# A graph-attention and mixture-of-experts block: one weight fetch for two dense batches, and a different order of begun pairs at the end

## The chip, the cores and the metric

The kernel runs on one core of one Trainium2 chip. The time is the device time of one launch in microseconds (us). The core has engines with queues of their own that run in program order: PE (matrix products), DVE (vector work), ACT (activation functions), POOL (small vector work and the DMAs whose row numbers are data), and SP (plain DMAs). They wait for each other through semaphores. SBUF is the on-chip memory; PSUM holds what PE writes, in eight banks of 128 x 512 numbers here.

## The reference, cut to what matters

`x` is 64 batches of 256 rows of 256 numbers. Two layers are applied to every batch:

- layer 0: `x += elu(attention with 4 heads over adj)` and then `x += layernorm(x) @ W.T + b`
- layer 1: `x += relu(attention with 1 head over adj)` and then a mixture of eight experts with two chosen for each row:

```python
logits = tokens @ router_w.T                 # 8 numbers per row
rw, re = top_k(softmax(logits), 2)           # two experts and two weights, made to sum to 1
out = tokens
for e in range(8):
    h = gelu(tokens @ w1[e] + b1[e])
    out = out + combine[:, e:e+1] * (h @ w2[e] + b2[e])
```

All is float32. Tokens are normalized before every attention, feed-forward and expert stage; the result is 64 x 256 x 256 numbers.

## The kernel before, in words

**Routed batches and dense batches.** The first 62 batches are "routed". After a batch's layers, each of its rows is written twice to a buffer in device memory (`xs`), once in the region of each chosen expert (`send`, L877, an indirect DMA on POOL). Rows of one expert are then taken up in *pairs* of 128-row tiles, 256 rows each (`expert_pair`, L710): the pair is loaded by four DMAs (L726) and a small one for its weights (`xt`, L737), the expert's first weights and bias are fetched (`we`, 288 KB, L752), DVE turns the rows (`turned`, L116), PE and ACT form the hidden values (`hidden`, L783 and L789), PE multiplies by the second weights, which stay in SBUF (`result`, L798), DVE adds the bias and copies PSUM to a buffer `y` (L804), ACT multiplies each row by its weight (L776), and POOL adds the rows to the result in device memory (`scatter`, L815: two accumulating indirect DMAs of 128 rows each). The scatters of a pair wait for those of the pair before, since the same row can be in both. There are 131 pairs; below they are counted from 0 to 130. The last 14 (the flush) hold the incomplete remainders of each region, filled up by rows that point to the last batch.

The last two batches, 62 and 63, are "dense" (`dense_expert`, L831): all eight experts are applied to all their rows, with weights that are zero for experts not chosen; sums stay in SBUF (`base`) and are stored once. There each expert's weights are fetched once for each of the two batches. The result of the second matrix product goes to a `y` buffer with the bias added, and is then added to `base` by two DVE instructions (L843). The store of batch 63 comes after all scatters, because filling rows are added there.

**The order of the work** is written out by a small planner (L1042 to L1078). It counts steps, and three steps (TICKS) make up the time of one batch. Every piece of work is a generator; in each step every active one is advanced once, in the order of the ranks it yielded (low first), and a negative rank means once more in the same step. The order of these calls is the program order on all queues. The rules that matter here:

- A new batch is begun at steps 2, 5, 8 and so on, the last at step 191; its layers take 19 steps. `more` becomes false at step 194.
- In steps with step mod 3 = 1, waiting pairs are begun, against a credit: 2.0 more at each such step while there are new batches, 3.0 after that, 3.0 at most in store.
- A pair is loaded in the step it is begun (rank 90), fetches weights one step later, is turned another step later (rank 95), has its hidden product two steps after that (rank 30), its result one step later (rank 80), and is scaled in the next (rank 2). One pending pair is scattered in each step (rank 97).
- Two dense experts are begun in each step with step mod 3 = 2.
- `later` holds back parts of the routing of a chunk to certain steps of the three.

**Buffers**: seven for `we`, five for a pair's rows `xr`, seven for `y`, twelve for `xt`. A `y` buffer is free again when its scatter has landed, so the DVE instruction L804 can have to wait for a scatter.

Of the kernel before, what the change touches and what calls it, by code (L numbers as in the profile page):

```python
# [27 lines left out]
def kernel(  # L28
# [17 lines left out]
    nc = tc.nc  # L46
    B, N, D = x.shape
    E = router.shape[0]
# [3 lines left out]
    NT = N // P  # L52
# [194 lines left out]


    C_B1, WROW = KT * D, KT * D + 64
    WBUFS, XBUFS, YBUFS = 7, 5, 7  # L250
    wpack = tc.dram_tile([E, P, WROW], F32, name="wpack")
    w2s = const.tile([P, E, KT * D], F32, tag="w2s", name="w2s")
    b2s = const.tile([P, E, D], F32, tag="b2s", name="b2s")
# [158 lines left out]
    def projected1(xT, rstd, b):  # L412

        q = q1s[b % 2]
        pqs = []
        for t in range(NT):
            pq = bank("pq", [D + 3])
            for k in range(KT):
                nc.tensor.matmul(  # L419
                    pq, xT[:, k, t * P : (t + 1) * P], wx1[:, k, :],  # L420
                    start=(k == 0), stop=(k == KT - 1),
                )
            pqs.append(pq)
        ex = small.tile([P, NT, 3], F32, tag="ex1", name="ex1")
        for t, pq in enumerate(pqs):
            nc.scalar.activation(ex[:, t, :], pq[:, D:], AF.Exp, scale=rstd[:, t : t + 1])
            nc.scalar.activation(
                q[:, t, :D], pq[:, :D], AF.Copy, scale=rstd[:, t : t + 1]
            )
        me = work.tile([P, NT, N], F32, tag="me", name="me")  # L430
        for j in range(NT):
            nc.scalar.activation(me[:, j, :], masks[1][:, j, :], AF.Copy, scale=ex[:, j, 0:1])
        return q, ex, me
# [276 lines left out]
    def expert_pair(j, n, ids, ef, regs, needs):  # L710

        i = j % GROUP
        upto = min(j + GROUP, n)
        if i == 0:
            _, regs["e"] = nc.values_load_multi_w_load_instructions(
                ids[0:1, 0, j:upto], engines=[mybir.EngineType.SP], min_val=0, max_val=E - 1,
                skip_runtime_bounds_check_because=WHY,
            )
            _, regs["t"] = nc.values_load_multi_w_load_instructions(
                ids[0:1, 1, j:upto], engines=[mybir.EngineType.SP], min_val=0, max_val=E * CAP,  # L720
                skip_runtime_bounds_check_because=WHY,
            )
        e_sp, t_sp = regs["e"][i], regs["t"][i]
        xr = io.tile([P, PAIR // S, KT * S], F32, tag="xr", name="xr", bufs=XBUFS)
        loads = [
            nc.sync.dma_start(  # L726
                out=xr[g * S : (g + 1) * S],
                in_=xs_d.rearrange("(t c q) f -> t q c f", c=PAIR // S, q=S)[
                    bass.ds(t_sp, 1), :, :, g * KT * S : (g + 1) * KT * S
                ].rearrange("t q c f -> (t q) c f"),  # L730
            )
            for g in range(P // S)
        ]

        xt = small.tile([P, 2, ROW - D], F32, tag="xt", name="xt", bufs=12)
# [14 lines left out]
        yield 90  # L750
        we = io.tile([P, WROW], F32, tag="we", name="we", bufs=WBUFS)
        nc.sync.dma_start(  # L752
            out=we, in_=wpack[bass.ds(e_sp, 1), :, :].rearrange("e p c -> (e p) c")
        )
        yield 95
        xT = turned(work.tile([P, KT, PAIR], F32, tag="sT", name="sT", bufs=3), xr)
        w = small.tile([P, 2], F32, tag="w", name="w", bufs=8)
# [15 lines left out]
        y = result(hT, bass.ds(regs["x"][i], 1))  # L773
        yield 2
        for t in range(2):
            nc.scalar.activation(y[:, t, :], y[:, t, :], AF.Copy, scale=w[:, t : t + 1])  # L776
        scatters.append((y, xt))
# [13 lines left out]
            )  # L791
        return hT

    def result(hT, e):
        py = bank("py", [2, D])
        for t in range(2):
            for f in range(KT):
                nc.tensor.matmul(  # L798
                    py[:, t, :], hT[:, f, t * P : (t + 1) * P],
                    w2s[:, e, f * D : (f + 1) * D].rearrange("p e c -> p (e c)"),  # L800
                    start=(f == 0), stop=(f == KT - 1),
                )
        y = io.tile([P, 2, D], F32, tag="y", name="y", bufs=YBUFS)
        nc.vector.tensor_add(y, py, b2s[:, e, :].to_broadcast([P, 2, D]))  # L804
        return y
# [22 lines left out]
            tc.add_to_no_dep_group("out", d.ins)  # L828
            added.append(d.ins)

    def dense_expert(b, e):  # L831

        own = dense_batch[b]
        yield 90
        we = io.tile([P, WROW], F32, tag="we", name="we", bufs=WBUFS)
        nc.sync.dma_start(out=we, in_=wpack[e])
        yield 40
        yield 30
        hT = hidden(own["xT"], we)
        yield 80  # L840
        y = result(hT, slice(e, e + 1))
        for t in range(NT):
            nc.vector.scalar_tensor_tensor(  # L843
                own["base"][:, t, :], y[:, t, :], own["w"][:, t, e : e + 1],
                own["base"][:, t, :], op0=ALU.mult, op1=ALU.add,
            )
        if e == E - 1:
            while b == B - 1 and (scatters or len(added) < 2 * PAIRS):
                yield 99
            d = nc.sync.dma_start(  # L850
                out=out_rows[b * N : (b + 1) * N, :].rearrange("(t p) d -> p t d", p=P),
                in_=own["base"],
            )
            before = added[-2:] + based if b == B - 1 else []
            tc.declare_no_dep(
                d.ins, query=SYNC, group="out", keep=before,
                reason="no row is added to here, or every add is in their chain",
            )
            for ins in before:
                tc.add_manual_dep(d.ins, ins.name, AFTER, reason="filling rows were added here")  # L860
            tc.add_to_no_dep_group("out", d.ins)
            nc.sync.nop()


    active = []
# [3 lines left out]
    def begin(job, rank):  # L869
        active.append([rank, len(order), job])  # L870
        order.append(job)
# [16 lines left out]
    def later(rank, *phases):  # L888

        yield rank  # L890
        while order_steps[-1] % TICKS not in phases:
            yield rank

    def route(c, row0, nt, n, last, xng, lg):
# [101 lines left out]
    def route_dense(b, lg):  # L996
# [11 lines left out]
        )  # L1008
        nc.vector.tensor_tensor(w, ohs[:, 0], ohs[:, 1], ALU.add)
        dense_batch[b]["w"] = w  # L1010
        dense_jobs.extend(lambda e=e: dense_expert(b, e) for e in range(E))

    FLUSH = 2 * (E - 1)
    PAIRS = ROUTED * NT + E - 1
# [1 line left out]
    def jobs():  # L1016
        b = done = taken = 0
        for c, nb in enumerate(CHUNKS + (1,) * DENSE):
            nt = nb * NT
            lg = keep.tile([P, nt, E], F32, tag="lg", name=f"lg_{c}", bufs=10)  # L1020
            xng = []
            row0 = b * N
            done += nt
# [13 lines left out]

    batches = jobs()
    step, more, credit = 2, True, 0.0
    SETUP_AT = 3  # L1040
    with tc.manual_schedule():
        while more or active or waiting or dense_jobs or scatters:  # L1042
# [5 lines left out]
                    begin(nxt, 25)  # L1048
            if step >= SETUP_AT and setup:
                begin(setup.pop(0)(), 90)  # L1050
            if phase == 1:
                credit = min(credit + (2.0 if more else 3.0), 3.0)
                while waiting and credit >= 1.0:
                    credit -= 1.0
                    begin(waiting.pop(0)(), 90)
            if phase == 2:
                for _ in range(2):
                    if dense_jobs:
                        begin(dense_jobs.pop(0)(), 90)
            if scatters:  # L1060
                def one():
                    scatter()
# [51 lines left out]
```

## Time and profile before

| | us |
|---|---|
| three runs, median (lowest to highest) | 1665.73 (1664.08 to 1666.54) |
| the profiled execution itself | 1670.08 |
| its span in the profile | 1668.3 |
| busy: PE, DVE, ACT, POOL | 1495.5, 1317.4, 833.2, 889.4 |
| last product of the layers (L599) ends | 1419.2 |
| last product of a pair (L798) ends | 1635.8 |
| last scatter (L815) is issued | 1660.1 |

Times in the profile count from the start of its span. A group of instructions is named by engine, line, and what it writes and reads. In views of waits, the number is the time for which the first engine sat idle until the second one released it. The chain is the work followed back from the last instruction, at each step to what released it. A DMA that an engine issues through its queue lands later than its issue ends.

### The profile page before, as it was taken

What the parts mean: (1) busy time and instruction counts of PE and PEld (TensorE: products, weight loads), DVE (VectorE), ACT (ScalarE), POOL (GpSimd) and SP (SyncE); (2) the same over time, 40 slices, a digit from 0 to 9 for tenths busy, and PEclk for the clock granted to TensorE, in tenths of its full rate; (3) what the DMA queues carried; (4) which work ended last, traced back from release to release, by engine and by line L of the source; (5) the groups of instructions that cost most, each with busy time, mean ns of one, the idle gap of its engine ahead of it and who ended that gap; (6) DMA issues with size and microseconds to landing.
All of it is one profiled execution on the core that took longest, in us unless ns stands there. A gap on an engine that the chain in (4) does not pass through costs nothing.

```text
span 1668.3 us, 30242 instructions
## 1 busy us (share of the span) xinstructions
PE 1495.5 (90%) x8474; PEld 1311.2 (79%) x8474; DVE 1317.4 (79%) x4478; ACT 833.2 (50%) x1832; POOL 889.4 (53%) x853
## 2 busy tenths in 40 slices
PE   5898888899999999999999999999989987678782
PEld 4777777688888888888888888888878876567671
DVE  6888989999898988898989898998889876423330
ACT  0243444455656666666666665655555565323221
POOL 0121433545757575757575757574764666444344
PEclk8999999999999999999999999999999998879986
DMA  3812223255757575756575766665564676866753
GB/s 107 231 41 58 61 70 94 74 142 114 167 118 163 118 159 129 140 132 146 133 149 134 145 133 146 137 140 121 123 142 99 115 156 141 200 135 112 155 107 44
DMA packets 365285, 209.74 MB, mean 126 GB/s; under 512 B 264376, under 2 KB 335040, under 8 KB 365120
## 3 DMA queue, kind: packets, MB, share of 16 engines
q1 hardware_dynamic: 314496, 139.43, 34.0%
q0 software_dynamic: 49632, 67.39, 22.5%
q8 instruction: 70, 1.15, 0.3%
q10 hardware_dynamic: 992, 0.99, 0.2%
q14 instruction: 95, 0.78, 0.2%
HBM read 118.55 MB, written 89.15 MB: 124 GB/s over the span
## 4 chain that ended last, share of the span: by engine, by line
PE 55%; DVE 26%; DMA 6%; issue 5%; POOL 4%; ACT 2%; SPq 1%; DVEq 0%; POOLq 0%; ACTq 0%
PE ph L783 14%; PE pv L475 12%; PE py L798 9%; PE pq L384 5%; PE pq L419 4%; DVE z L461 4%; PE pf L529 4%; DVE stats L353 4%; DMA out_dram<-y,xt 3%; PE pt L368 3%; POOL out_dram L815 2%; DVE mv L354 2%; PE pl L599 2%; PE pd L454 1%; DVE x L535 1%
## 5 line engine op out<-in xcount | busy, mean ns | idle before, releaser
L815 POOL DMA_INDIRECT out_dram<-y,xt x262 | 416.7, 1591 | 255.4 <-DMA out_dram<-y,xt 73.0
L475 PE MATMUL pv<-q,z 128*128 128x65 f32 (+1 forms) x2560 | 369.8, 299 | 6.7 <-DVE z L461 5.3
L475 PEld LDWEIGHTS pv<-q,z 128*128 128x128 f32 x2560 | 331.9, 194 | 19.5 <-DVE z L461 5.8
L783 PE MATMUL ph<-sT,we 128*128 128x256 f32 x1048 | 259.1, 405 | 56.2 <-DVE sT L116 47.1
L361 POOL TENSOR_SCALAR rstd<-mv 128x4 f32<-128x4 f32 (+1 forms) x132 | 69.7, 528 | 436.1 <-DVE mv L354 352.9
L877 POOL DMA_INDIRECT xs<-xng,pos x248 | 251.1, 1012 | 69.2 <-issue 66.9
L783 PEld LDWEIGHTS ph<-sT,we 128*128 128x128 f32 x1048 | 209.8, 205 | 90.9 <-DVE sT L116 50.6
L798 PE MATMUL py<-w2s,hT 128*128 (+1 forms) x1176 | 263.9, 379 | 1.4 <-DVE z L461 0.7
L798 PEld LDWEIGHTS py<-w2s,hT 128*128 128x128 f32 x1176 | 219.7, 190 | 29.7 <-DVE z L461 1.0
L374 ACT COPY xT<-pt 128x512 f32<-128x512 f32 x192 | 113.3, 590 | 222.4 <-PE pt L368 184.7
L804 DVE TENSOR_TENSOR y<-py,b2s 128x512 f32<-128x512 f32 x147 | 97.5, 688 | 158.9 <-PE py L798 88.7
L789 ACT ACTIVATE hT<-ph,we 128x256 f32<-128x256 f32 x294 | 122.8, 471 | 183.3 <-PE ph L783 80.9
L461 DVE SCALAR_TENSOR_TENSOR z<-pd,q,mask 128x256 f32<-128x256 f32 x512 | 211.1, 473 | 0.3 <-PE pd L454 0.2
L362 POOL TENSOR_TENSOR rstd<-rstd,mhalf 128x4 f32<-128x4 f32 (+1 forms) x132 | 162.6, 1232 | 11.0
L776 ACT ACTIVATE y<-y,w 128x256 f32<-128x256 f32 x262 | 113.1, 501 | 104.4 <-DVE y L804 96.3
L353 DVE BATCH_NORM_STATS2 stats<-x 128x6 f32<-128x256 f32 x384 | 156.3, 407 | 2.2
L384 PE MATMUL pq<-wx,xT 128*128 128x268 f32 x512 | 137.9, 415 | 8.6 <-DVE wt L257 4.2
L419 PE MATMUL pq<-wx,xT 128*128 128x259 f32 x512 | 129.1, 394 | 15.5 <-ACT xT L374 11.2
L529 PE MATMUL pf<-wfT,xT 128*128 128x256 f32 x512 | 125.0, 388 | 0.0
L419 PEld LDWEIGHTS pq<-wx,xT 128*128 128x128 f32 x512 | 91.9, 189 | 41.9 <-ACT xT L374 22.4
L384 PEld LDWEIGHTS pq<-wx,xT 128*128 128x128 f32 x512 | 100.9, 202 | 30.1 <-issue 6.9
L551 ACT ACTIVATE rel<-pv,rinv 128x256 f32<-128x256 f32 x128 | 54.0, 474 | 108.2 <-DVE rinv L482 95.8
(151 smaller groups left out, 2233.8 us busy)
## 6 DMA issues: line engine op xcount, KB each, us to landing
we<-wpack SPq DMA_DIRECT2D x147, 288.0 KB
xr<-xs SPq DMA_DIRECT2D x524, 64.0 KB
xblk<-in_x_dram SPq DMA_DIRECT2D x256, 64.0 KB
xin<-in_x_dram SPq DMA_DIRECT2D x64, 256.0 KB
out_dram<-base SPq DMA_DIRECT2D x64, 256.0 KB
out_dram<-y,xt POOLq DMA_INDIRECT x262
xs<-xng,pos POOLq DMA_INDIRECT x248
xs<-fill SPq DMA_DIRECT2D x9, 260.0 KB
```

The source lines that it names most:

```text
L353: nc.vector.bn_stats(stats[:, t, :], src[:, t, :])
L362: nc.gpsimd.tensor_tensor(rstd[:, :n], rstd[:, :n], mhalf[:, :n], ALU.pow)
L384: nc.tensor.matmul(pq.rearrange("p h c -> p (h c)"), xT[:, k, t * P : (t + 1) * P], wx[:, k, :], start=(k == 0), stop=(k == KT - 1),)
L419: nc.tensor.matmul(pq, xT[:, k, t * P : (t + 1) * P], wx1[:, k, :], start=(k == 0), stop=(k == KT - 1),)
L461: nc.vector.scalar_tensor_tensor(z[:, j, :], pd[:, i, :], q[:, j, h, d + 2 : d + 3], mask[:, j, :], op0=ALU.max, op1=ALU.mult,)
L475: nc.tensor.matmul(pv[:, h, :], z[:, j, t * P : (t + 1) * P], q[:, j, h, : d + 1], start=(j == 0), stop=(j == NT - 1),)
L529: nc.tensor.matmul(pf[:, t, :], xT[:, k, t * P : (t + 1) * P], wfT[:, k, :], start=(k == 0), stop=(k == KT - 1),)
L783: nc.tensor.matmul(ph[:, f, :], we[:, k * D + f * P : k * D + (f + 1) * P], xT[:, k, :], start=(k == 0), stop=(k == KT - 1),)
L789: nc.scalar.activation(hT[:, f, :], ph[:, f, :], AF.Gelu, bias=we[:, C_B1 + f : C_B1 + f + 1])
L798: nc.tensor.matmul(py[:, t, :], hT[:, f, t * P : (t + 1) * P], w2s[:, e, f * D : (f + 1) * D].rearrange("p e c -> p (e c)"), start=(f == 0 ...
L815: d = nc.gpsimd.indirect_dma_start(out=out_rows, out_offset=bass.IndirectOffsetOnAxis(ap=xt[:, t, 0:1].bitcast(I32), axis=0), in_=y[:, t, ...
L877: d = nc.gpsimd.indirect_dma_start(out=xs_d[: E * CAP * PAIR, :], out_offset=bass.IndirectOffsetOnAxis(ap=at, axis=0), in_=xe, in_offset=None,
```

## The change

It has five parts. (1) A dense expert is one piece of work for both dense batches: one weight fetch, and then hidden product and result of batch 62 and, one step later, of batch 63. The jobs are begun once both batches are routed, one at every even step, instead of two at every third step. (2) Their results are not copied to `y`: DVE adds the PSUM product and the bias to `base` directly, in four instructions a batch and expert. The stores become jobs of their own. (3) From step 180 (DRAIN_AT) credit for pairs grows by 3.0, no longer from step 194. From step 209 (QUIET) one pair is begun in every step if fewer than three pairs wait for their scatter. (4) When there are no new batches, the turn of a pair has rank 75 rather than 95, and routing is no longer held back by `later`. (5) Buffers: `y` 7 to 9, `xt` 12 to 14, `w` 8 to 12, `me` 2 to 1, `lg` 10 to 7.

```diff
-    WBUFS, XBUFS, YBUFS = 7, 5, 7
+    WBUFS, XBUFS, YBUFS = 7, 5, 9
...
-        me = work.tile([P, NT, N], F32, tag="me", name="me")
+        me = work.tile([P, NT, N], F32, tag="me", name="me", bufs=1)
...
-        yield 95
+
+        yield 95 if more else 75
         xT = turned(work.tile([P, KT, PAIR], F32, tag="sT", name="sT", bufs=3), xr)
...
-    def result(hT, e):
+    def product(hT, e):
         py = bank("py", [2, D])
...
+        return py
+
+    def result(hT, e):
+        py = product(hT, e)
         y = io.tile([P, 2, D], F32, tag="y", name="y", bufs=YBUFS)
...
-    def dense_expert(b, e):
-
-        own = dense_batch[b]
+    def dense_expert(e):
+
         yield 90
         we = io.tile([P, WROW], F32, tag="we", name="we", bufs=WBUFS)
         nc.sync.dma_start(out=we, in_=wpack[e])
         yield 40
...
+        for b in range(ROUTED, B):
+            own = dense_batch[b]
+            yield 35
+            hT = hidden(own["xT"], we)
+            yield -85
+            py = product(hT, slice(e, e + 1))
+            for t in range(NT):
+                for add in (py[:, t, :], b2s[:, e, :]):
+                    nc.vector.scalar_tensor_tensor(
+                        own["base"][:, t, :], add, own["w"][:, t, e : e + 1],
+                        own["base"][:, t, :], op0=ALU.mult, op1=ALU.add,
+                    )
+            if e == E - 1:
+                begin(store_dense(b), 99)
...
-        while order_steps[-1] % TICKS not in phases:
+        while more and order_steps[-1] % TICKS not in phases:
...
-        dense_jobs.extend(lambda e=e: dense_expert(b, e) for e in range(E))
+        if b == B - 1:
+            dense_jobs.extend(lambda e=e: dense_expert(e) for e in range(E))
...
-            lg = keep.tile([P, nt, E], F32, tag="lg", name=f"lg_{c}", bufs=10)
+            lg = keep.tile([P, nt, E], F32, tag="lg", name=f"lg_{c}", bufs=7)
...
+    DRAIN_AT, QUIET = TICKS * (B - 4), TICKS * B + 17
...
-            if phase == 1:
-                credit = min(credit + (2.0 if more else 3.0), 3.0)
+            if step >= QUIET:
+                if waiting and len(scatters) < 3:
+                    begin(waiting.pop(0)(), 90)
+            elif phase == 1:
+                credit = min(credit + (2.0 if step < DRAIN_AT else 3.0), 3.0)
                 while waiting and credit >= 1.0:
                     credit -= 1.0
                     begin(waiting.pop(0)(), 90)
-            if phase == 2:
-                for _ in range(2):
-                    if dense_jobs:
-                        begin(dense_jobs.pop(0)(), 90)
+            if dense_jobs and step % DENSE == 0:
+                begin(dense_jobs.pop(0)(), 90)
```

More of the change, by code (lines that the diff above doesn't have):

```diff
@@ L733, in expert_pair @@
         ]
-        xt = small.tile([P, 2, ROW - D], F32, tag="xt", name="xt", bufs=12)
+        xt = small.tile([P, 2, ROW - D], F32, tag="xt", name="xt", bufs=14)
         loads.append(
@@ L754, in expert_pair @@
         )
-        yield 95
+        yield 95 if more else 75
         xT = turned(work.tile([P, KT, PAIR], F32, tag="sT", name="sT", bufs=3), xr)
-        w = small.tile([P, 2], F32, tag="w", name="w", bufs=8)
+        w = small.tile([P, 2], F32, tag="w", name="w", bufs=12)
         yield 30
@@ L837, in dense_expert @@
         yield 40
[L838 to L862, printed above, removed]
+        for b in range(ROUTED, B):
[12 more added lines that the diff above has]
+                begin(store_dense(b), 99)
@@ new lines, in store_dense @@
+    def store_dense(b):
+        own = dense_batch[b]
+        yield 99
+        while b == B - 1 and (scatters or len(added) < 2 * PAIRS):
+            yield 99
+        d = nc.sync.dma_start(
+            out=out_rows[b * N : (b + 1) * N, :].rearrange("(t p) d -> p t d", p=P),
+            in_=own["base"],
+        )
+        before = added[-2:] + based if b == B - 1 else []
+        tc.declare_no_dep(
+            d.ins, query=SYNC, group="out", keep=before,
+            reason="no row is added to here, or every add is in their chain",
+        )
+        for ins in before:
+            tc.add_manual_dep(d.ins, ins.name, AFTER, reason="filling rows were added here")
+        tc.add_to_no_dep_group("out", d.ins)
+        nc.sync.nop()
```

## The prediction

> **What bounds the kernel now.** I began with the busy shares over time (40 slices of 41.7 us, tenths):
>
> ```profile
> PE   5898888899999999999999999999989987678782
> ...
> DVE  6888989999898988898989898998889876423330
> ```
>
> Through slice 31 PE and DVE are full; in the last seven neither is, and in the last nothing is. The table by stage says when (columns: stretch, length, then busy time and instructions of PE, weight loads, DVE, ACT, POOL, granted clock, DMA share, GB/s):
>
> ```profile
> 1225.00:1320.00 95.00, 91.90 (x524) 81.41 (x523) 85.37 (x317) 54.25 (x117) 55.18 (x53) 0.96 0.52 109
> 1320.00:1430.00 110.00, 87.40 (x409) 75.24 (x408) 78.65 (x357) 59.01 (x124) 70.37 (x66) 0.89 0.74 160
> 1430.00:1636.00 206.00, 164.85 (x688) 139.75 (x688) 68.66 (x165) 64.43 (x146) 89.26 (x58) 0.89 0.67 128
> 1636.00:1668.30 32.30, 0.00 (x0) 0.00 (x0) 0.63 (x1) 0.91 (x2) 12.35 (x8) 0.58 0.35 45
> ```
>
> From 1430 on only pairs and dense experts are left, 238 us, and PE has 41 us of slack before its last product and then 32 us without work. So who sets the end? POOL's list in order of time, at its undisturbed end:
>
> ```profile
> 1651.90 1.54 POOL L815 DMA_INDIRECT out_dram<-y,xt  x1 [2.97 <-DMA out_dram<-y,xt]
> 1653.75 1.54 POOL L815 DMA_INDIRECT out_dram<-y,xt  x1 [0.30 <-issue]
> 1658.29 1.54 POOL L815 DMA_INDIRECT out_dram<-y,xt  x1 [2.99 <-DMA out_dram<-y,xt]
> ```
>
> A pair issues two scatters (1.85 apart), and the next pair starts 4.54 later, when they have landed: about 6.4 us a pair. From 1429.50 to 1658.29, in that list, 33 pairs start, 32 gaps, mean 7.15. Twenty-six gaps are 6.36 to 7.23 (mean 6.80; the 18 of them before 1600, with loads beside them, mean 6.92); six are 7.9 to 9.6. So the scatter chain sets the tail almost alone. The six long gaps show in the waits from 1430 to the end (total us, times, longest):
>
> ```profile
> POOL out_dram L815 <- DMA out_dram<-y,xt: 40.4, 12, 4.8
> PE ph L783 <- DVE sT L116: 39.6, 8, 9.8
> ...
> DVE y L804 <- DMA out_dram<-y,xt: 28.1, 8, 6.2
> ```
>
> and how they arise in the chain, in order of time (start, us, what):
>
> ```profile
> 1482.70 3.83 DMA out_dram<-y,xt
> ...
> 1486.65 0.70 DVE y L804
> ...
> 1489.69 0.72 DVE sT L116
> 1490.45 9.89 PE ph L783 x37
> ```
>
> A dense result wants a `y` buffer that a scatter still holds; the turns of the next three pairs stand behind it on DVE, PE starves and cools, the next pairs come late.
>
> [...] the trace has 2.97 after the issue has ended, and that is what I use. [...] 463 (L535) and 475 (L461) from PSUM, 482 (L843) from SBUF. [...] 24 hidden products take 5.45 us after 2.38 to 3.02 us idle, 8.28 after 9.83, but also 8.45 after 3.18.
>
> **The change, part by part.**
>
> *Pairs ahead.* I counted the planner's steps with the rules above. At step 178 two chunks become due, 12 pairs wait at step 179, and both kernels begin 3 at step 181. At steps 184, 187, 190 and 193 the old kernel begins 2 each, the new 3 each: 4 pairs more. At 196 to 208 both begin 3 every third step. So in step 209 the old kernel scatters pair 98 (its 1429.50), the new one pair 102. After it the old one has 32 pairs to scatter, one a step (last in step 241), the new one 28 (last in 238, with step 222 empty).
>
> *What the four pairs cost earlier.* Each is 8 + 8 products, 1.81 + 1.78 = 3.6 us of PE (5.45/3, 5.34/3), and 0.69 (L804) + 0.69 (L116) + 0.37 (L762, L766) = 1.75 us of DVE. They fall into 1225 to 1320, where PE has 3.1 us of slack in 95 and DVE 9.6. Between 4 x 1.75 = 7 us (PE's busy time there is stretched by waits: earlier batches take 21.4 us between base stores, these 24) and 4 x 3.6 = 14; I take 11. POOL gets 4 x 3.4 us of issue more; its own slack covers that in sum (55 of 95 busy), but it runs in order, and a norm can stand behind a waiting scatter, as here, where `rstd` is on the chain right behind one:
>
> ```profile
> 1350.36 1.55 POOL out_dram L815
> 1351.92 0.29 POOL rstd L361
> 1352.28 0.74 POOL rstd L362
> 1353.04 0.87 DVE x L535 x2
> ```
>
> Bounds: 0, and 4 x 6.45 = 26 if each extra scatter's cycle lengthens the layers; I take 3.
>
> *Routing not held, turns first.* From step 194 the routing steps move up by one or two (the fills from step 209 to 207). From 1320 to 1430 PE idles 22.6 us, largely because turns (rank 95) stand behind a chunk's small DVE instructions (1420.3 to 1427.6 is one such row, PE idle 6.84 before 1431.36). With rank 75 they stand ahead. Between 0 and 12 us back (nothing, or half the idle time; POOL's chain needs 6.45 of each of these steps of 8.4 us); I take 5. A turn ahead of L804 adds one wait: if rows are late, `y`, the scale and the scatter are late too. The load is two steps, 13 us, earlier and a load lands in 2 to 5 us, so 0; without that cover, the lateness goes straight into the chain.
>
> *The dense experts.* Eight fetches of 288 KB less, 2.36 MB, 18 us at 128 GB/s, in the shadow of other DMAs; eight SP issues fewer, with SP at some 3 us of each step (four row loads 1.9, `xt` 0.4, `we` 0.5, in SP's list). DVE per batch and expert: before 0.69 + 2 x 0.48 = 1.65, after 2 x 0.47 + 2 x 0.48 = 1.90; sixteen times, +4 us, hidden (DVE busy 69 of 206 us). They no longer take `y` buffers, and there are nine: PE may be nine pairs ahead of the scatters, where now it is seven buffers shared with the dense results. So the 28.1 us of DVE and with it the long gaps should go; the gap becomes that of an undisturbed pair with loads beside it, 6.92. Ends: 6.45 (undisturbed by loads) and 7.15 (as now).
>
> *One pair a step.* Does PE keep up? From step 209 it has 26 pairs and 16 dense units, 42 x 3.6 = 151 us at full clock, 170 at the 0.89 of now; 28 gaps of 6.92 are 194. In steps 215 to 230, with both, it needs 7.2 us for 6.92, so it gives back some 4 us of its lead of about 18 (two triples, 43 us of scatters in steps 209 to 214 for 22 us of PE). Covered.
>
> *Buffers.* `me` single: ACT writes (L432) at 1342.17 and next at 1360.54, DVE reads within a step of the first: 0; without that cover ACT, and the scales behind it, would wait part of a step. `lg`, `xt`, `w`: 0, their releases lie many steps back. A dense `we` lives 3 to 4 steps, so two of them and four of pairs take 6 of 7 buffers: no wait for SP, with the loads of the next pair queued behind it; a wait there would cost up to a step once.
>
> *Sum, against the profiled execution's span:* 1429.5 + 11 + 3 - 5 = 1438.5 for pair 102; + 28 x 6.92 = 193.8 gives 1632.3 for the start of pair 130; + 10.0 as now (1658.29 to 1668.3: second scatter, landing, store) = 1642.3. The median of the runs is 2.6 below this span, so 1639.7: **1640**, 1.5% faster. The likeliest case's own range is 1627 to 1651 (12 us either way: 7 to 14 for the pairs, 6.7 to 7.1 for the gap).
>
> **The rivals.**
>
> *The shift is worth more* (0.15): the layers cover the four pairs, turns give back 12, gaps of 6.6: 1429.5 + 0 + 185 + 10 - 2.6 = 1622. For it: PE and DVE idle from 1320. Against: before 1320 they don't.
>
> *The gap stays 7.15 and the layers pay all* (0.22): 1429.5 + 14 + 3 + 200 + 10 - 2.6 = 1654. For it: denser DMA traffic beside the scatters, 0.95 MB in each step of 7 us. Against: the six long gaps alone make up the 11 us by which the 32 exceed 6.80 each.
>
> *Slower* (0.10): POOL, in steps 184 to 208, with three scatters a batch. If in each of those eight batches a norm waits a whole scatter cycle, 6.45, the layers last 8 x 6.45 = 52 us longer: 1429.5 + 52 + 194 + 10 - 2.6 = 1683. It decides from about 35 us, 4.4 a batch. For it: the four lines above. Against: batches with three pairs today (the base stores at 1205.75 and 1230.20, 24.45 apart) last no longer than their neighbours (24.16, 24.19).
>
> *It doesn't matter* (0.03): the lead is lost again at PE, below a clock of 0.78, where 151 us become 194: 1663 to 1669. Now it is 0.89 with long idle times, which should shrink.
>
> **How the numbers follow.** The forecast has 0.50. Faster by over 0.2% (about what a measurement of this kernel can tell from no change) are the first three: 0.87; same 0.03; slower 0.10. For eight in ten I leave out the slower and unchanged cases and the lower half of the best: 1620 to 1660.
>
> **What would show it.** Right: pair 102 or so scattered when the last layer product ends; gaps near 6.9 with no run of 8 to 9; L804 hardly waiting for the scatter DMA; PE's waits for `sT` below 10 us in the tail; 139 fetches of `we`. Wrong: base stores over 27 us apart from 1250 on with POOL between them; gaps above 7.3; PE at a low clock. If SP turns out to wait for buffers in the tail, the loads bound the chain, and I have missed that.

## The result, and the profile after

| | before | after |
|---|---|---|
| median of four runs each, us (lowest to highest) | 1665.3 (1664.08 to 1666.54) | 1648.61 (1645.09 to 1651.53) |
| the profiled execution / its span | 1670.08 / 1668.3 | 1651.53 / 1649.6 |
| last `base` of batch 56 / of batch 63 (L574) | 1253.27 / 1400.89 | 1249.90 / 1416.02 |
| last product of the layers (L599) ends | 1419.2 | 1427.0 |
| first scatter of pair 102 / 119 / 130 | 1459.44 / 1583.74 / 1658.29 | 1443.07 / 1569.05 / 1639.68 |
| span's end after the last of these | 10.0 | 9.9 |

The ratio of the times is 0.9897, with a 95% interval of 0.9884 to 0.9911: 1.0% faster, where 1.5% was forecast. The two profiled executions lie further apart than the medians, since that of the kernel before took 4.8 us more than its median, that of the kernel after 2.9. Batches and pairs are counted from 0; `base` of a batch is what its layers hand to the routing, so its time marks the end of that batch's layers.

The busy shares over time of the kernel after (40 slices of 41.2 us, tenths of each slice; PEclk is the granted clock):

```profile
PE   5898888999999999999999999999989997599930
...
DVE  6888989999898989898989898999988877545510
...
PEclk8999999999999999999999999999999998799965
```

The dip of PE has moved to the slice at the end of the layers (5), and behind it PE is full until its work is finished. The table by stage (columns as before):

```profile
1225.00:1320.00 95.00, 93.19 (x525) 83.05 (x526) 85.79 (x306) 53.96 (x118) 52.53 (x50) 0.96 0.61 128
1320.00:1430.00 110.00, 88.44 (x441) 76.11 (x440) 78.63 (x361) 60.81 (x128) 77.32 (x70) 0.91 0.71 155
1430.00:1636.00 206.00, 140.16 (x636) 121.72 (x635) 71.74 (x169) 58.84 (x133) 90.78 (x59) 0.85 0.63 112
1636.00:1649.60 13.60, 0.00 (x0) 0.00 (x0) 0.00 (x0) 0.00 (x0) 3.69 (x3) 0.50 0.33 53
```

PE's clock of 0.85 from 1430 is a mean over work and idle time. The scatters of the tail split it better: the first row below runs from pair 102 to pair 119, the second from there to pair 130.

```profile
1443.07:1569.05 125.98, 124.80 (x569) 108.89 (x568) 62.48 (x149) 49.68 (x112) 52.80 (x35) 0.99 0.75 145
1569.05:1639.68 70.63, 11.85 (x55) 10.08 (x54) 4.90 (x12) 7.05 (x16) 33.95 (x23) 0.60 0.36 41
```

In the first row PE is busy 99% of the time at a granted clock of 0.99, and yet it isn't what most of the scatters wait for. L799 issues 280 products in it and 32 after it, eight to a result: 16 dense results and 19 of pairs in the first row, 4 of pairs after it. So 23 of pairs are left to multiply when 28 pairs are left to scatter, and 4 when 11 are left. PE draws away from POOL while it is full.

The waits of the kernel after from 1430 to the end (total us, times, longest):

```profile
POOL out_dram L820 <- DMA out_dram<-y,xt: 64.8, 19, 5.4
...
DVE y L809 <- DMA out_dram<-y,xt: 10.0, 2, 5.7
...
PE ph L784 <- DVE y L809: 9.6, 1, 9.6
```

The first line can't be set against the 40.4 of before. The view puts many of the waits of a scatter down to whatever else ended at that moment, even to loads of weights (`we`, 8.4 in the kernel after) that a scatter doesn't use, and a second profile of the same kernel has 48.5 in this line. Under all names together POOL's waits before L820 are 118.8 us here and 134.9 before; the gaps between scatters, below, are the better measure. DVE's wait for a `y` buffer has fallen from 28.1 to 10.0, and PE's for the turn `sT` (39.6 before) is no longer among the large ones: 2.2 us, once, before 1442.

POOL in order of time, in the loaded part and at the end:

```profile
1503.35 1.54 POOL L820 DMA_INDIRECT out_dram<-y,xt  x1 [3.32 <-DMA out_dram<-y,xt]
1505.19 1.54 POOL L820 DMA_INDIRECT out_dram<-y,xt  x1 [0.31 <-issue]
1511.12 1.54 POOL L820 DMA_INDIRECT out_dram<-y,xt  x1 [4.38 <-ACT hT L790]
...
1633.21 1.54 POOL L820 DMA_INDIRECT out_dram<-y,xt  x1 [2.93 <-DMA out_dram<-y,xt]
1635.06 1.54 POOL L820 DMA_INDIRECT out_dram<-y,xt  x1 [0.30 <-issue]
1639.68 1.54 POOL L820 DMA_INDIRECT out_dram<-y,xt  x1 [3.07 <-DMA out_dram<-y,xt]
```

The pair at 1503.35 needs 7.77 us, the one at 1633.21 needs 6.47. The gaps from 102 to 119 have a mean of 7.41 (125.98/17), those from 119 to 130 of 6.42 (70.63/11). In the kernel before the same pairs have 7.31 and 6.78 (124.30/17 and 74.55/11). So only the last eleven gaps have become shorter, those that now run when PE's work is done.

**Where the 18.7 us between the spans come from.** Batch 56 is 3.4 earlier (1253.27 to 1249.90; the second profile of the kernel after, below, has 1246.18, so this term is uncertain by that much). From there to the last `base` the layers take 166.1 instead of 147.6: 18.5 lost. From the last `base` to pair 102 there are 27.05 instead of 58.55: 31.5 gained. The chain from 102 to 130 takes 196.6 instead of 198.85: 2.2 gained. The end is 0.1 shorter. Sum 3.4 - 18.5 + 31.5 + 2.2 + 0.1 = 18.7. So the lead in pairs pays, and more than half of it is paid for in the layers. What makes them 15 us later?

### The profile page after: what moved, and what is told of

Read it like the earlier page. It is cut to its first block, busy times and chain, and to the rows that moved or that the text cites. A ratio compares the mean times of both kernels' runs of the same rounds, so it can differ in the third digit from the quotient of the medians.

```text
span 1649.6 us, 30216 instructions
## 1 busy us (share of the span) xinstructions
PE 1476.3 (89%) x8474; PEld 1299.8 (79%) x8474; DVE 1323.8 (80%) x4494; ACT 831.0 (50%) x1832; POOL 889.4 (54%) x853
## 3 DMA queue, kind: packets, MB, share of 16 engines
q0 software_dynamic: 49632, 67.39, 22.8%
## 4 chain that ended last, share of the span: by engine, by line
PE 62%; DVE 21%; DMA 5%; POOL 4%; issue 3%; ACT 3%; SPq 1%; DVEq 0%; POOLq 0%; ACTq 0%
PE pv L475 14%; PE ph L784 13%; PE py L799 12%; PE pq L384 5%; PE pq L419 5%; PE pf L529 4%; DVE z L461 3%; PE pt L368 3%; DVE stats L353 3%; DMA out_dram<-y,xt 3%; POOL out_dram L820 2%; PE pl L599 2%; DVE mv L354 2%; ACT xT L374 1%; PE pd L454 1%
## 5 line engine op out<-in xcount | busy, mean ns | idle before, releaser
L820 POOL DMA_INDIRECT out_dram<-y,xt x262 | 415.4, 1585 | 241.1 <-DMA out_dram<-y,xt 87.6
L361 POOL TENSOR_SCALAR rstd<-mv 128x4 f32<-128x4 f32 (+1 forms) x132 | 71.0, 538 | 432.2 <-DVE mv L354 337.1
L799 PE MATMUL py<-w2s,hT 128*128 (+1 forms) x1176 | 266.1, 379 | 1.3 <-ACT hT L790 1.2
L784 PE MATMUL ph<-sT,we 128*128 128x256 f32 x1048 | 242.8, 385 | 11.8 <-DVE y L809 9.6
L799 PEld LDWEIGHTS py<-w2s,hT 128*128 128x128 f32 x1176 | 219.5, 190 | 30.0 <-ACT hT L790 2.2
L784 PEld LDWEIGHTS ph<-sT,we 128*128 128x128 f32 x1048 | 198.9, 194 | 38.5 <-issue 9.9
L461 DVE SCALAR_TENSOR_TENSOR z<-pd,q,mask 128x256 f32<-128x256 f32 x512 | 211.1, 473 | 0.3 <-PE pd L454 0.2
L362 POOL TENSOR_TENSOR rstd<-rstd,mhalf 128x4 f32<-128x4 f32 (+1 forms) x132 | 163.0, 1235 | 11.0
L809 DVE TENSOR_TENSOR y<-py,b2s 128x512 f32<-128x512 f32 x131 | 85.8, 686 | 68.6 <-PE py L799 48.8
L529 PE MATMUL pf<-wfT,xT 128*128 128x256 f32 x512 | 124.1, 386 | 0.0
```

Of the source, the lines that this page charges most:

```text
L362: nc.gpsimd.tensor_tensor(rstd[:, :n], rstd[:, :n], mhalf[:, :n], ALU.pow)
L461: nc.vector.scalar_tensor_tensor(z[:, j, :], pd[:, i, :], q[:, j, h, d + 2 : d + 3], mask[:, j, :], op0=ALU.max, op1=ALU.mult,)
L529: nc.tensor.matmul(pf[:, t, :], xT[:, k, t * P : (t + 1) * P], wfT[:, k, :], start=(k == 0), stop=(k == KT - 1),)
L784: nc.tensor.matmul(ph[:, f, :], we[:, k * D + f * P : k * D + (f + 1) * P], xT[:, k, :], start=(k == 0), stop=(k == KT - 1),)
L799: nc.tensor.matmul(py[:, t, :], hT[:, f, t * P : (t + 1) * P], w2s[:, e, f * D : (f + 1) * D].rearrange("p e c -> p (e c)"), start=(f == 0 ...
L820: d = nc.gpsimd.indirect_dma_start(out=out_rows, out_offset=bass.IndirectOffsetOnAxis(ap=xt[:, t, 0:1].bitcast(I32), axis=0), in_=y[:, t, ...
```

## The experiments

The theory after this reading: the four pairs cost the layers time because POOL runs in order, and the small norm instructions (`rstd`, L361 and L362) stand behind their waiting scatters. Its rival: the pairs' products and turns take the time of PE and DVE, as the forecast had it. A second dispute: what shortens the tail, the lead or the single edits to its order, buffers and fetches. A ratio is that to the kernel before on the same chip, with its 95% interval; all edits are to the changed kernel.

### One repeat, and the early drain undone

**The changed kernel again**, unedited:

> The changed kernel itself, as the measure for the other runs of this series: ratio to the kernel before 0.988 to 0.991, last base (ACT, L574) 14 to 16 us later than in the kernel before. Both theories expect the same.

Measured: 1649.9 us, ratio 0.990 (0.9873 to 0.9926). In its profile the marks are 1.0 to 3.7 us earlier: batch 56 1246.18, last `base` 1412.93, pair 102 1441.55, pair 130 1638.66. Differences of that size between two profiles are not read as effects below. It is the yardstick for the profiles below.

**No early drain**, all else as changed:

```diff
-    DRAIN_AT, QUIET = TICKS * (B - 4), TICKS * B + 17
+    DRAIN_AT, QUIET = TICKS * B + 2, TICKS * B + 17
```

> The changed kernel, but three pairs a batch only from step 194 on, as before; step 209 then scatters pair 98 rather than 102. Theory (the lead of four pairs is what pays): the tail has 32 gaps instead of 28, 28 us more, and the layers lose 11 to 18 us less: 10 to 17 us slower than the changed kernel, 1658 to 1666. Rival (the layers pay the lead back, and the gain comes from the dense experts having left the y buffers): within 3 us of the changed kernel's 1648.6.

Measured: 1656.3, ratio 0.9929 (0.9906 to 0.9951), span 1656.9. The last `base` is at 1395.01, and pair 102 at 1452.86. So the early drain moves pair 102 by 9.8 (1452.86 to 1443.07): from the last `base` to pair 102 it saves 30.8 (57.85 to 27.05), and the layers give back 21.0 (1395.01 to 1416.02). The chain from 102 to 130 takes 194.2 here against 196.6, which leaves 7.3 between the spans and about 5 between the medians' ratios, whose intervals just overlap; by time alone its worth is barely shown. The drain isn't the whole of the gain: without it the kernel is 11.4 us of span below the one before, of which 4.0 lie before batch 56, 1.8 in the layers after it, 0.6 from the last `base` to pair 98, 4.8 in the chain from pair 98 to 130 (228.8 to 224.0), and 0.2 at the end.

### What the four pairs cost: scatters or products

**The same four pairs (86, 89, 92, 95), not scattered.** They are loaded, turned and multiplied; their rows are not added to the result.

```diff
+        begun.append(j)
+        mine = len(begun) - 1
...
-        scatters.append((y, xt))
+        if mine not in SKIP:
+            scatters.append((y, xt))
...
+    begun, SKIP = [], (86, 89, 92, 95)
```

> The changed kernel, with the scatters of pairs 86, 89, 92 and 95 left out (the third pair of four batches; their rows are missing in the result), all their other work kept. Theory (in the last batches the layers wait for POOL, whose queue is held by one scatter cycle in every step, and with it for sends and norms): the last base comes 12 to 20 us earlier than in the changed kernel, and the time falls by as much. Rival (the extra products and vector work are the price): 0 to 5 us earlier.

**The same four pairs, scattered but without products.** Their `y` is zeroed by DVE instead.

```diff
-        hT = hidden(xT, we)
+        hT = hidden(xT, we) if mine not in SKIP else None
...
-        y = result(hT, bass.ds(regs["x"][i], 1))
+        if mine in SKIP:
+            y = io.tile([P, 2, D], F32, tag="y", name="y", bufs=YBUFS)
+            nc.vector.memset(y, 0.0)
+        else:
+            y = result(hT, bass.ds(regs["x"][i], 1))
```

> The changed kernel, with the products and activations of the hidden layer and the result of pairs 86, 89, 92 and 95 left out; a DVE memset of y stands in for L809, loads, scales and scatters stay. Theory (POOL is the price): the last base moves by less than 5 us. Rival (PE is the price, 4 x 3.6 us): 9 to 15 us earlier, and the time falls by as much.

Measured: without scatters 1633.59, ratio 0.9798 (0.9777 to 0.9819); without products 1652.68, ratio 0.9918 (0.9901 to 0.9936), no faster than the repeat beside them. The last `base` in ACT's list in order of time, in the repeat:

```profile
1412.93 1.08 ACT L574 ACTIVATE base<-x,by 128x256 f32<-128x256 f32 x2
```

without scatters:

```profile
1397.15 1.08 ACT L574 ACTIVATE base<-x,by 128x256 f32<-128x256 f32 x2
```

and without products:

```profile
1413.83 1.08 ACT L574 ACTIVATE base<-x,by 128x256 f32<-128x256 f32 x2
```

So leaving out the products ends the layers no earlier, and leaving out the scatters ends them 15.8 us earlier, 4 a pair. Pair 102 comes 15.8 earlier too (1425.79), and the time is 16.3 lower: the whole of it reaches the end. The chain of the kernel after shows how (start, us, what):

```profile
1355.69 1.61 POOL out_dram L820
1357.30 0.30 issue
1357.60 1.58 POOL out_dram L820
1359.19 0.29 POOL rstd L361
...
1359.55 0.74 POOL rstd L362
...
1360.31 0.88 DVE x L535 x2
```

and the waits near the end of the layers (1330 to 1420) count it. The kernel before:

```profile
DVE by L560 <- POOL rstd L362: 6.7, 3, 4.4
...
DVE x L535 <- POOL rstd L362: 2.5, 1, 2.5
```

The repeat:

```profile
DVE by L560 <- POOL rstd L362: 16.3, 3, 8.3
...
DVE x L535 <- POOL rstd L362: 7.3, 2, 5.9
```

Without the products:

```profile
DVE by L560 <- POOL rstd L362: 16.7, 3, 8.8
...
DVE x L535 <- POOL rstd L362: 10.6, 2, 8.2
```

Without the scatters:

```profile
DVE by L560 <- POOL rstd L362: 7.0, 2, 6.9
```

DVE's wait for `rstd` falls from 23.6 to 7.0 us when the scatters go, and stays (27.3) when the products go: 16.6 us, near the 15.8 by which the layers end earlier.

That is not the whole of the price, though. Cut at the `base` of batch 60, the layers after batch 56 show two stretches (columns as before). The kernel before:

```profile
1253.27:1344.42 91.15, 87.08 (x506) 77.33 (x505) 78.93 (x296) 53.28 (x115) 53.79 (x52) 0.98 0.54 113
1344.42:1400.89 56.47, 47.47 (x219) 40.93 (x218) 40.25 (x190) 32.83 (x70) 37.79 (x37) 0.88 0.77 160
```

The kernel after:

```profile
1249.90:1347.58 97.68, 96.29 (x562) 86.20 (x561) 86.24 (x315) 58.88 (x130) 59.62 (x56) 1.00 0.61 129
1347.58:1416.02 68.44, 49.88 (x243) 42.53 (x241) 42.58 (x213) 32.83 (x72) 48.45 (x44) 0.90 0.68 137
```

Without the four scatters:

```profile
1245.76:1343.44 97.68, 96.29 (x562) 86.23 (x561) 86.92 (x318) 58.94 (x130) 57.89 (x57) 1.00 0.61 128
1343.44:1397.15 53.71, 46.68 (x243) 41.21 (x241) 41.48 (x213) 33.02 (x71) 38.24 (x37) 0.96 0.75 157
```

Without the products:

```profile
1246.68:1341.83 95.15, 88.56 (x513) 78.01 (x511) 85.09 (x316) 55.77 (x121) 58.49 (x55) 0.98 0.62 127
1341.83:1413.83 72.00, 49.73 (x228) 42.33 (x227) 43.40 (x215) 32.94 (x71) 50.89 (x47) 0.87 0.71 138
```

Of the 18.5 us that the layers lose, 6.5 are lost before batch 60 and 12.0 after it. Before batch 60 PE is busy for 96.29 of 97.68 us at a granted clock of 1.00, with 9.2 us more of work than in the kernel before; leaving out the scatters changes nothing there, and leaving out the products shortens the stretch by 2.5; what the other 4.0 are is not shown. After batch 60 the scatters decide: DVE waits 21.9 us for `rstd` (15.9 and 6.0) instead of 9.2, 12.7 more, near the 12.0. The time won without products before batch 60 is lost again behind the scatters (72.00), so it doesn't show at the end of the layers. The two prices don't add up: with the scatters gone, the layers after batch 56 still take 151.4 us, against 147.6 in the kernel before and 145.8 without the early drain.

**The norms taken off POOL**, the cause in another way: all scatters stay, but from step 194 on `rstd` is formed by ACT as exp(-0.5 ln(variance + eps)), with `eps_c` a constant tile.

```diff
+        if order_steps and order_steps[-1] >= TICKS * B + 2:
+            nc.scalar.activation(rstd[:, :n], mv[:, :n, 1], AF.Ln, bias=eps_c)
+            nc.scalar.activation(rstd[:, :n], rstd[:, :n], AF.Exp, scale=-0.5)
+            return
```

> The changed kernel, with the two POOL instructions of a norm (L361, L362) replaced from step 194 on by two on ACT, exp(-0.5 ln(var + eps)); each brings up to two table loads of 1.28 us, and ACT was busy 47 of 80 us between 1320 and 1400. Theory (of POOL's price, most comes from norms that stand behind a scatter waiting for its turn): DVE no longer waits for rstd for 16 + 7 us between 1330 and 1420, the last base comes 5 to 14 us earlier, and the time falls by 3 to 12 us. Rival (sends that stand behind scatters are the price, and pair loads wait for them): the last base within 4 us of the changed kernel's, or later by ACT's loads.

Measured: 1641.17, ratio 0.9848 (0.9828 to 0.9869), which lies below the changed kernel's interval (0.9884 to 0.9911): the fastest here that leaves nothing out. The last `base` of this kernel:

```profile
1395.95 1.10 ACT L580 ACTIVATE base<-x,by 128x256 f32<-128x256 f32 x2
```

It is 17 us earlier than in the repeat, with all four pairs scattered, and DVE waits for no `rstd` from 1330 to 1442. This run takes all late norms from behind all scatters, not only those of the four pairs, and the norms' own time off POOL; the kernel before with its norms off POOL was not run. That the four pairs' scatters are the cause rests on the run without them; this one adds that it is the order on POOL rather than the scatters' traffic, which is all still there. Only half comes out at the end: pair 102 at 1434.94 is 6.6 earlier. POOL still has the same sends and scatters in its order, and PE now waits for weights (19.0 us for `we` from 1330 to 1442); which of the two holds the rest back was not tested. The rest is 2.8 us in the chain (102 to 130 takes 194.35). The table by stage of this kernel shows what fills the time:

```profile
1320.00:1400.00 80.00, 74.36 (x387) 65.26 (x386) 66.11 (x306) 69.60 (x136) 57.34 (x48) 0.98 0.74 151
```

The changed kernel's row of the same stretch:

```profile
1320.00:1400.00 80.00, 67.35 (x347) 58.46 (x346) 58.72 (x260) 46.77 (x101) 59.01 (x54) 0.94 0.67 140
```

PE gets 7 us more work done in these 80, and ACT, with room before, takes up 22.8 us more: more work in the stretch, the norms, and a table load of 1.28 us each for the logarithm and the exponential.

### Is the tail the scatter chain's?

**One scatter a pair from pair 102 on**, so the second 128 rows of each of these pairs are not added.

```diff
-        for t in range(2):
+        scattered.append(y)
+        for t in range(2 if len(scattered) <= 102 else 1):
```

> The changed kernel, with only the first of the two scatters of each pair from pair 102 on (half of their rows are missing in the result). Theory (the scatter chain sets the whole tail): the undisturbed gap falls from 6.43 by the 1.85 between the two issues to about 4.6, and the time by 40 to 52 us, until PE's last product (1581) plus some 12 us is reached. Rival (PE or the loads set the part of the tail with dense experts, where the chain of the profile runs through PE from 1442 to 1574): 15 to 25 us less, from the last eleven gaps alone.

Measured: 1598.5, ratio 0.959 (0.9555 to 0.9625), 51 us below the repeat. POOL in order of time:

```profile
1537.91 1.54 POOL L821 DMA_INDIRECT out_dram<-y,xt  x1 [5.37 <-ACT y L777]
1544.82 1.54 POOL L821 DMA_INDIRECT out_dram<-y,xt  x1 [5.36 <-ACT y L777]
...
1563.81 1.54 POOL L821 DMA_INDIRECT out_dram<-y,xt  x1 [3.64 <-ACT y L777]
1568.26 1.54 POOL L821 DMA_INDIRECT out_dram<-y,xt  x1 [2.91 <-ACT hT L790]
1572.75 1.54 POOL L821 DMA_INDIRECT out_dram<-y,xt  x1 [2.95 <-ACT hT L790]
```

With one scatter an undisturbed gap is 4.45 to 4.49. (This kernel was timed twice only, 1594.99 and 1602.01.) The gaps around 1540 are 6.91, and end with the scaling of `y`, which has to wait for products: there PE has become the bound, with a pair and a dense unit in each gap (busy 28.00 of the 28.00 us from 1531 to 1559). So the chain bounds the tail of the changed kernel, but PE stands only 0.5 us a gap behind it (6.91 against 7.41).

### The single parts, undone one at a time

**Two fetches again** (one for each dense batch, the second a step later):

```diff
-        for b in range(ROUTED, B):
+        we2 = io.tile([P, WROW], F32, tag="we", name="we", bufs=WBUFS)
+        nc.sync.dma_start(out=we2, in_=wpack[e])
+        for b, we in zip(range(ROUTED, B), (we, we2)):
```

> The changed kernel, with the dense weights fetched twice again, 8 x 288 KB more while scatters run. Theory (scatters land later when loads run beside them, 7.2 to 7.4 a gap against 6.43; what the single fetch saves is in that): 2.36 MB more beside 17 loaded gaps, about a seventh more load traffic, so a seventh of their 16 us of excess: 1 to 4 us slower. Rival (the fetches are hidden): within 1 us. Third possibility (SP waits for a free weight buffer and pair loads come late behind it): 5 us or more slower.

Measured: 1647.18, ratio 0.9891 (0.9868 to 0.9915). The table of this kernel for the stretch with dense work:

```profile
1430.00:1570.00 140.00, 129.53 (x587) 112.98 (x588) 68.11 (x159) 53.57 (x121) 58.65 (x38) 0.96 0.82 163
```

and of the changed one:

```profile
1430.00:1570.00 140.00, 129.26 (x587) 112.46 (x587) 67.74 (x161) 52.15 (x118) 58.39 (x38) 0.96 0.75 146
```

The DMA share is 0.82 instead of 0.75, at 163 GB/s instead of 146, and from 102 to 119 it takes 124.1 against 126.0. The fetch saved is worth nothing that these runs can tell, and its bytes don't set the gap.

**Dense results through `y` again**, and, in another kernel, **seven `y` buffers**:

```diff
-            py = product(hT, slice(e, e + 1))
+            y = result(hT, slice(e, e + 1))
...
-                for add in (py[:, t, :], b2s[:, e, :]):
-                    nc.vector.scalar_tensor_tensor(
-                        own["base"][:, t, :], add, own["w"][:, t, e : e + 1],
-                        own["base"][:, t, :], op0=ALU.mult, op1=ALU.add,
-                    )
+                nc.vector.scalar_tensor_tensor(
+                    own["base"][:, t, :], y[:, t, :], own["w"][:, t, e : e + 1],
+                    own["base"][:, t, :], op0=ALU.mult, op1=ALU.add,
+                )
```

> The changed kernel, but dense results go through a y buffer (one bias addition, two additions to base) as before; nine buffers, one weight fetch for both batches. Theory of the prediction (dense results in the y buffers made the long gaps): 4 to 10 us slower, DVE waiting for the scatter DMA over 25 us in the tail. Rival (with the pairs one a step and nine buffers it does not matter, DVE stalls are hidden by PE's lead): within 2 us.

```diff
-    WBUFS, XBUFS, YBUFS = 7, 5, 9
+    WBUFS, XBUFS, YBUFS = 7, 5, 7
```

> The changed kernel with seven result buffers instead of nine. Theory (the scatter chain bounds, PE is far ahead, and dense results no longer take buffers): within 2 us of 1648.6. Rival (the two buffers are needed to keep the chain fed): 4 us or more slower, with DVE waiting for scatters for over 25 us in the tail.

Measured: 1648.68, ratio 0.989 (0.986 to 0.992), and 1651.6, ratio 0.9902 (0.9877 to 0.9926). The waits from 1430 on in the kernel with dense results through `y`:

```profile
DVE y L809 <- DMA out_dram<-y,xt: 48.8, 11, 7.9
```

and in the kernel with seven buffers:

```profile
DVE y L809 <- DMA out_dram<-y,xt: 40.6, 9, 6.4
```

These waits are longer than the 28.1 of the kernel before and the 15.7 of the repeat. Pair 130 starts at 1638.58 and 1639.02 all the same (1638.66 in the repeat). With a lead, DVE's wait for a buffer was here the scatter chain pushing back, not what made it slow.

**Turns last again**, **routing held again**, and **groups of three to the end**:

```diff
-        yield 95 if more else 75
+        yield 95
```

> The changed kernel, but the turn of a pair keeps rank 95. Theory of the prediction (turns first give back 5 us): 3 to 8 us slower than 1648.6. Rival (a turn that waits for late rows holds up the bias addition behind it, and the layers): 2 to 6 us faster.

```diff
-        while more and order_steps[-1] % TICKS not in phases:
+        while order_steps[-1] % TICKS not in phases:
```

> The changed kernel, but routing is held to its steps to the end, as before. Theory (the layers end 15 us later because sends and routing crowd together on POOL and DVE in the last batches, and pair loads then wait for fresh sends): base (ACT, L574) of the last batch 4 us or more earlier than 1416, and 3 to 8 us faster than 1648.6. Rival (three scatters a batch are the cause): the last base stays within 3 us of 1416, and the time stays within 3 us or grows by one step, 7 us.

```diff
-    DRAIN_AT, QUIET = TICKS * (B - 4), TICKS * B + 17
+    DRAIN_AT, QUIET = TICKS * (B - 4), TICKS * B + 999
```

> The changed kernel, but pairs are begun three at a time at every third step to the end, as before. Step count: the last pair is scattered in step 237 rather than 238. Theory (the scatter chain sets the tail as long as it is fed, whatever the order of begun pairs): within 3 us of the changed kernel. Rival (beginning one a step is what removes the long gaps): 5 us or more slower, with several gaps over 8 us between 1480 and 1600 as in the kernel before.

Measured: 1654.19, ratio 0.9902 (0.987 to 0.9934); 1652.49, ratio 0.9906 (0.9881 to 0.9931); 1650.81, ratio 0.9914 (0.9884 to 0.9945). The last `base` stands at 1415.95, 1414.66 and 1414.52 (the kernel after 1416.02), pair 130 at 1645.51, 1638.98 and 1636.22. None of the three is told from the changed kernel by its time. In the profile of the first the tail is 6 us longer, which its ratio doesn't bear out.

## Why the prediction was right, and where it was not

The direction and the order of the gain were right: 1648.61 is within 1620 to 1660 and within the likeliest case's own 1627 to 1651, 8.6 above 1640. Against the sum's own terms: pair 102 at 1443.1 for 1438.5 (+4.6), 28 gaps of 7.02 for 6.92 (+2.8), the end 9.9 for 10.0, and the median 1.0 below the profiled span instead of 2.6 (+1.6). The sum of these is 8.9.

Part of this closeness is luck. The 9 us that the sum allowed for the layers (11 + 3 - 5) were 18.5 from batch 56 on, 9.5 more. They became +4.6 because batch 56 came 3.4 earlier, which was not forecast, and because the way from the last `base` to the pair at this place was 1.6 shorter (28.61 to 27.05).

- **Pairs ahead: held.** After the layers' last product the new kernel goes on to scatter pair 100, the old one pair 97: three ahead by the clock, four by the count of steps, in which 102 stands where 98 had.
- **"What the four pairs cost earlier": the terms were the wrong way round.** 3 for POOL was 15.8, by the run without scatters. The 11 for PE and DVE has an answer only in part: up to batch 60, where PE is full, 6.5 us are lost and the scatters have no share in them, but without the products the layers end no earlier, because the scatters' delay covers that. The likeliest case had named the mechanism, a norm behind a waiting scatter, and its bound of 0 to 26 held the value, but "its own slack covers that in sum" failed: POOL was idle for 32.7 of the 110 us from 1320 to 1430 in the kernel after, and still the four pairs' scatters delayed norms: DVE waited 23.6 us for `rstd` in the repeat and 7.0 without them. The rival "slower" priced the same mechanism at 6.45 in each of eight batches; measured, the layers lose 18.5 in all, 2.3 for each of its eight batches, below the 4.4 where it would have decided. The mark given for it, base stores more than 27 apart, isn't there either: 25.2 at most. The delay is uneven: 1.2 to 2.5 us a batch up to batch 60, 6.4 in the next one.
- **"I take 5" for turns first and routing not held: not found.** Undoing either leaves the last `base` within 1.4 us. The idle time of PE from 1320 to 1430 is 21.6 against 22.6. More of it hangs on POOL and the norms than on the rank of the turns: from 1320 to 1400 PE idles 12.7 us in the changed kernel and 5.6 with the norms off POOL.
- **The gap of 6.92: the rule failed, the size nearly held.** The mark "gaps above 7.3" came in the loaded part (7.41), 6.42 came in the unloaded part, and the mean of 7.02 lay between the ends of 6.45 and 7.15. That the mean of two kinds of gap comes near the 6.92 for all is luck. The long gaps did not go with DVE's waits: from pair 98 on there are seven of 7.9 or more, six before. Their explanation by `y` buffers falls with the two kernels above, which have more of those waits and no longer tail.
- **The dense experts and one pair a step at nothing: held.** There are 139 fetches of `we`, and neither the second fetch nor groups of three change the time. DVE's additions to `base` took 481 ns each with the product from PSUM and 485 with the bias from SBUF; in the kernel before the means are 464 and 473 for L535 and L461 with a source in PSUM, and 482 for L843 from SBUF.
- **PE keeps up: held, for a smaller lead.** It was to lose 4 us of an 18 us lead to gaps of 6.92; since the gaps were 7.41 it gained. At 6.92 it would have been level with the 6.91 that the kernel with one scatter shows for it.
- **SP waiting for buffers: not found as such**, but the loads of pairs wait for fresh rows: 31.0 us in 1330 to 1442 for the sends (`xs`), 10.6 before in a longer stretch (1180 to 1435). Fewer pairs are in store, and the sends stand behind the same scatters; that this is the reason was not tested.
- **Sums and readings.** Three need a correction, and none moves the forecast. The sum of the rival "worth more" leaves out the 12 us that it says the turns give back; with them it comes to 1610. The lead of two triples is 43 - 22 = 21 us, not 18. And the lines on 24 hidden products leave out four triples of the kernel before: 7.74 us after 6.84 idle, 7.23 after 9.07 and 7.81 after 7.30 (granted clock 0.70, 0.75 and 0.69), but also, at 1623.53, 7.13 after 2.38 (0.76), where others took 5.45 after as long (1.00). So an idle time under 3 us did not always leave PE fast here.

Open: whether a pair's scatters could start before those of the pair before have landed, since every kernel here is written to wait (2.97 to 2.99 us of idle POOL at the undisturbed end of the one before); why the loaded gap is 7.4 rather than the 6.4 of the end, when more bytes don't lengthen it; how the 11.4 us of span that the kernel without the early drain still gains are shared among the other parts, as each single part undone is less than these runs resolve; and with that the 3.4 to 7.8 us by which every variant is earlier by batch 56. From batch 51 to 56 all of them need 118.1 to 120.4 us and the kernel before 124.0, but of that kernel there is one profile, and the early drain can't be the reason, since the variant without it needs 120.0. The kernel without scatters shows what removing the four pairs' scatters would be worth, but draining still earlier with norms off POOL was not run.

## What to carry to other kernels

Work brought forward into a busy stage was priced here by what its instructions stood in front of on an in-order queue, not by whether that engine had idle time in sum: four pairs' scatters cost 15.8 us on an engine that was busy 64% of that stretch before (70.37 of 110 us). Products added to a full PE lengthened the stretch in which they ran (97.68 us with them, 95.15 without), but this did not show at the end of the layers, since the scatters set the stretch behind it (68.44 us with both, 72.00 without the products, 53.71 without the scatters). If a chain at the end is the bound, look at the small critical instructions that share its queue first: moving the norms to an engine with room gave 8.7 us more. A long wait for a buffer that a bounding chain holds was back-pressure: 48.8 and 40.6 us of it left the start of pair 130 within 0.4 us of the repeat's. So before adding buffers, see whether the chain's own gaps end with that wait.

## What the runs showed of the hardware

- An indirect DMA that waited on POOL held up the small arithmetic queued behind it there: of 23.6 us of DVE waiting for `rstd`, 16.6 went when four pairs' scatters were left out.
- A dependent accumulating scatter of 128 rows took 4.45 to 4.49 us from start to start, a pair of them 6.42 undisturbed (1.85 for the second issue), and 7.4 with loads and products beside it, although a rise from 146 to 163 GB/s added nothing (124.1 us for 17 gaps, against 126.0).
